# Seven block products instead of eight in the expert layers of a mixture-of-experts stage

## The chip, the core and the metric

The kernel runs on one core of a Trainium2 chip. A core has a matrix engine (TensorE, "PE" in the profile), three engines for elementwise work (VectorE "DVE", ScalarE "ACT", GpSimd "POOL"), a queue that issues transfers (SyncE, "SP") and 16 DMA engines that carry all transfers. Each engine works through its own queue in order and waits there, by semaphores, for what it needs from others. Matmuls read on-chip memory (SBUF) and write accumulators (PSUM); GpSimd does not read PSUM. The metric is the device time in microseconds (us).

## The reference

Inputs: `x` with 4 x 512 tokens of 256 features, one condition vector per sequence. The result is `x` plus a linear attention over the output of a mixture of experts, plus a further branch (attention with a field term, then two layers of local attention and feed-forward). The change touches the experts alone:

```python
gate = xn @ wg_W + wg_b + (genre_embed @ gg_W + gg_b)
gate_w = jax.nn.softmax(gate, axis=-1)
topk_w, topk_i = jax.lax.top_k(gate_w, TOP_K)              # 2 of 8 experts per token
...
h1 = jax.nn.relu(jnp.einsum('bsh,ehm->bsem', x, W1) + b1)    # 256 -> 512
h2 = jax.nn.relu(jnp.einsum('bsem,emn->bsen', h1, W2) + b2)  # 512 -> 512
out_e = jnp.einsum('bsen,enh->bseh', h2, W3) + b3            # 512 -> 256
return jnp.einsum('bseh,bse->bsh', out_e, cw)
```

Everything is 32-bit floating point.

## The kernel before

The kernel computes an expert only for the tokens routed to it. After the gate it sorts the 4096 (token, expert) pairs by expert into **slots**. A slot has one or two blocks of 128 rows of one expert. `SLOTS` gives the order of their sizes: 1, 2, 2, 1, 2, 2, then three times 1, 2, 2, 2, then 1, 2, 2, 1: 22 slots that always run (`often`), 15 of two blocks and 7 of one, numbered here from 0. Two more one-block slots run under a condition and do not run with these inputs. `rowtok` holds for each row of a slot which token to fetch, `goal` which row of the DRAM scratch `ys` its result goes to; rows that hold no token go to row 0 of `ys`, which nobody reads.

For slot j the helpers are:
- `loads` (L1429): SP reads the expert's number and issues three weight loads, `w1` (516 KB, with the biases), `w2` (1024 KB) and `w3` (640 KB, with the output bias). Each has two buffers, so slot j+1's go into those of slot j-1.
- `gather` (L1440): an indirect transfer per block on POOL's queue (L1444) fetches the rows of `x` into `xb`; PE transposes them, ACT or DVE copies them to `xbT`.
- `layer` (L1458): a matrix layer. Weights are the stationary operand in pieces of 128 x 128, tokens the moving operand, 256 wide for two blocks, 128 wide for one. `relu` (L1418) adds the bias and clips at zero on the way out of PSUM, on ACT (L1420) and DVE (L1422) in turn. Each 32-bit product shows in the profile as two weight loads and two matmul instructions, all under L82.
- `last` (L1477): the third layer with the roles exchanged (activations stationary, weights moving, 256 wide), a DVE addition of the output bias (L1483) and an indirect transfer per block on POOL's queue (L1488), which scatters rows to `ys`. As all scatters write `ys`, each waits for the one before it to land.

The loop at L1506 is a software pipeline. Iteration j issues: first layer of j, `last` of j-1, loads and gather of j+1, one weight load for a later stage, second layer of j. Only the transposes and those late loads have a written order (`PE.in_order`, `tc.keep_in_program_order`, "pinned" below); for the rest a planner that knows the dependences chooses each engine's order, and it also moves work of later stages into idle time, such as the additions to `xres` at L1579 and the fills of `v` at L311 and L312, both on POOL. PSUM has four banks for the layers ("mm"), two for transposes, two for the third layer.

After the loop (L1549 on), `ys` is read back and weighted into `y`, four tiles of 128 x 1024 allocated at the start of the kernel and unused until then.

Of the kernel before, what the change touches and what calls it, by code (L numbers as in the profile page):

```python
# [12 lines left out]
F32 = mybir.dt.float32  # L13
I32 = mybir.dt.int32
AF = mybir.ActivationFunctionType
ALU = mybir.AluOpType
# [4 lines left out]
NT = S // 128  # L21
# [21 lines left out]
NRARE = 2  # L43
NROWT = 2 * NPAIR + NHALF
NHI = 2 * NROWT
MCONST = (128, 128 + NE, 2 * NE, 2, NE * NE, NHI, 2 * B * NT, 64, NE)
NMC = sum(MCONST)


# [18 lines left out]
def adaln_attn_ffn_kernel(ctx: ExitStack, tc: tile.TileContext, a: dict, out: bass.AP):  # L68
# [55 lines left out]
    def evac(dst, src):  # L124
        turn[0] ^= 1
        if turn[0]:
            nc.scalar.copy(dst, src)  # L127
        else:
            nc.vector.tensor_copy(dst, src)
# [1032 lines left out]
    with ExitStack() as abc:  # L1162
# [7 lines left out]
        with ExitStack() as moe:  # L1170
# [17 lines left out]
            for n in MCONST:  # L1188
                parts.append(mc[:, at : at + n])
                at += n  # L1190
            mtri, mtiles, mthr, mslot, mlow, miota, mtok, mfold, mwt = parts


            ys = dr.tile([1 + 2 * B * S, H], F32, tag="ys", name="ys")
            xall = a["x"].rearrange("b s h -> (b s) h")


# [201 lines left out]
            pmap2 = acct("pmap2")  # L1399
            for q in range(2):  # L1400
                PE.matmul(pmap2[64 * q : 64 * q + 64, :NROWT], mfold, half_map[:, :, q], start=True, stop=True)
            goal = xp.tile([128, NROWT], I32, tag="goal", name="goal")
            nc.vector.tensor_copy(goal, pmap2[:, :NROWT])
            rowtok = xp.tile([128, NROWT], I32, tag="rowtok", name="rowtok")
            nc.vector.tensor_scalar(rowtok, pmap2[:, :NROWT], -1.0, 0.0, ALU.add, ALU.max)
            nc.vector.tensor_single_scalar(rowtok, rowtok, B * S - 1, op=ALU.bitwise_and)


            def busy(n):
# [7 lines left out]

            def relu(dst, src, bias):  # L1418
                if turn[0]:
                    nc.scalar.activation(dst, src, AF.Relu, bias=bias)  # L1420
                else:
                    nc.vector.tensor_scalar(dst, src, bias, 0.0, ALU.add, ALU.max)  # L1422


            def place(kind, i):
# [11 lines left out]
                d.w3 = ew.tile([128, 5, H], F32, tag="w3", name="w3")  # L1437
                nc.sync.dma_start(d.w3, we[:, 8 + 6 * ME :].rearrange("p (c m) -> p c m", m=H))

            def gather(j, d):  # L1440
                xb = hp.tile([128, 2, H], F32, tag="xb", name="xb", bufs=3)
                for i in range(d.n):
                    r = place(d.n, SLOTS[j][0]) + i
                    nc.gpsimd.indirect_dma_start(  # L1444
                        out=xb[:, i, :], out_offset=None, in_=xall,
                        in_offset=bass.IndirectOffsetOnAxis(ap=rowtok[:, r : r + 1], axis=0))
                n = d.n * 128
                pt = tpt("pxb")
                with PE.in_order():
                    for c in range(2):  # L1450
                        for i in range(d.n):
                            PE.transpose(pt[:, c * n + i * 128 : c * n + (i + 1) * 128],
                                         xb[:, i, c * 128 : (c + 1) * 128], ident)
                xbT = hp.tile([128, 2, 256], F32, tag="xbT", name="xbT")
                evac(xbT[:, :, 0:n], pt[:, : 2 * n].rearrange("p (c t) -> p c t", t=n))
                d.xbT = xbT

            def layer(d, src, tag, w, bias):  # L1458
                n = d.n * 128
# [14 lines left out]
                        relu(dst[:, m, 0:n], ps[:, i * n : (i + 1) * n], d.w1[:, bias + m : bias + m + 1])  # L1474
                return dst

            def last(j, d):  # L1477
                ps = acct("po")
                for i in range(d.n):
                    mm(ps[:, i * H : (i + 1) * H],  # L1480
                       [(d.h2[:, c, i * 128 : (i + 1) * 128], d.w3[:, c, :]) for c in range(4)])
                ob = hp.tile([128, 2, H], F32, tag="ob", name="ob", bufs=3)
                nc.vector.tensor_tensor(  # L1483
                    ob[:, 0 : d.n, :], ps[:, : d.n * H].rearrange("p (i h) -> p i h", h=H),
                    d.w3[:, 4, :].unsqueeze(1).to_broadcast([128, d.n, H]), ALU.add)
                for i in range(d.n):
                    r = place(d.n, SLOTS[j][0]) + i
                    nc.gpsimd.indirect_dma_start(  # L1488
                        out=ys, out_offset=bass.IndirectOffsetOnAxis(ap=goal[:, r : r + 1], axis=0),
                        in_=ob[:, i, :], in_offset=None)  # L1490


            later = {
# [5 lines left out]
            cond_weights(wp, lambda name, load: later.update({name: load}))  # L1499
            cw_ = {}  # L1500

            ds = [SimpleNamespace() for _ in SLOTS]
            loads(0, ds[0])
            gather(0, ds[0])
            often, rare = ds[:-NRARE], range(len(ds) - NRARE, len(ds))
            for j, d in enumerate(often):  # L1506
                if j == len(often) - 1:
                    aside = conditions(cw_, wp)
                    next(aside)
                if j == len(often) - 2:  # L1510
                    halves = nc.values_load(nhalf[0:1, 0:1], min_val=0, max_val=2 * NE)
                if j == 1:
                    weights()
                h1 = layer(d, d.xbT, "h1", d.w1[:, 8:].rearrange("p (c m) -> p c m", m=ME), 0)
                if j:
                    last(j - 1, ds[j - 1])
                if j + 1 < len(often):
                    loads(j + 1, ds[j + 1])
                    gather(j + 1, ds[j + 1])
                    if j > 1 and later:  # L1520
                        name, behind[0] = next(iter(later)), True
                        cw_[name] = later.pop(name)()
                        behind[0] = False
                d.h2 = layer(d, h1, "h2", d.w2, 4)
            last(len(often) - 1, often[-1])

            next(aside)
# [1 line left out]
            with tc.If(halves > NHALF - NRARE):  # L1529
                for j in rare:  # L1530
                    d = ds[j]
                    loads(j, d)
                    gather(j, d)
                    h1 = layer(d, d.xbT, "h1", d.w1[:, 8:].rearrange("p (c m) -> p c m", m=ME), 0)
                    d.h2 = layer(d, h1, "h2", d.w2, 4)
                    last(j, d)
# [213 lines left out]
def _shape_constants():  # L1750
    f = np.float32
    p = np.arange(128)
    bmask = np.repeat((p[:, None] // 32 == p[None, :] // 32).astype(f)[:, None, :], 4, axis=1)
    hmask = np.where(p[:, None] // CHD == np.arange(8)[None, :], CHD**-0.5, 0.0)
    hmask = np.concatenate([hmask, p[:, None] // CHD % 2 == np.arange(2)[None, :]], axis=1).astype(f)
    i, j = p[:, None], p[None, :]
    lmask = np.concatenate([np.where(j >= i, 0.0, MASKED), np.where(j <= i, 0.0, MASKED)], axis=1).astype(f)

    kmask = np.concatenate([(j >= i % 64)[:, :64], (j <= i % 64)[:, :64], j >= i], axis=1).astype(f)

    e = np.arange(NE)
    thr = np.concatenate([256 * e + 128, 256 * e])
    slot = np.full((128, 2), -1)
    slot[: len(SLOTS), 0] = [i if n == 2 else NPAIR + i // 2 for i, n in SLOTS]
    slot[: len(SLOTS), 1] = [-1 if n == 2 else i for i, n in SLOTS]
    tile, expert = p // NE, p % NE
    mconst = np.concatenate(
        [(p[:, None] < p[None, :]).astype(f),
         ((tile[:, None] < tile[None, :]) & (expert[:, None] == expert[None, :])).astype(f),
         (expert[:, None] == e[None, :]).astype(f), np.tile(thr, (128, 1)).astype(f), slot.astype(f),  # L1770
         np.tile((e[None, :] <= e[:, None]).reshape(-1), (128, 1)).astype(f), np.tile(np.arange(NHI), (128, 1)).astype(f),
         (np.arange(2 * B * NT)[None, :] * 128 + p[:, None] + 1).astype(f),
         (p[:, None] % 64 == np.arange(64)[None, :]).astype(f),
         np.tile(np.where(e == NE - 1, 1 - NE, 1), (128, 1)).astype(f)], axis=1)

    pos = np.arange(S, dtype=f)
    inv = f(10000.0) ** np.repeat(np.arange(0, H, 2, dtype=f) / f(H), 2)
    peT = np.ascontiguousarray(np.sin(pos[:, None] / inv[None, :]).astype(f).T)

    half = np.arange(0, DHD, 2, dtype=f)  # L1780
    freqs = pos[:, None] * (f(1.0) / f(10000.0) ** (half / f(DHD)))[None, :]
    base = (half + f(0.4 * DHD)) / f(1.4 * DHD)
    scale = base[None, :] ** ((pos - f(S // 2)) / f(WIN // 2))[:, None]
    cos, sin = np.cos(freqs).astype(f), np.sin(freqs).astype(f)
    parts = []
    for sc in (f(8.0) * scale, f(1.0) / scale):
        c, s = cos * sc, sin * sc
        parts += [np.concatenate([c, c], 1), np.concatenate([-s, s], 1)]
    rot = np.stack(parts).astype(f).reshape(4, NT, 128, DHD).transpose(2, 0, 1, 3)
    return {"mconst": mconst, "bmask": bmask, "hmask": hmask, "lmask": lmask, "kmask": kmask, "peT": peT, "rot": rot}  # L1790
# [81 lines left out]
```

## Time and profile before

| | |
|---|---|
| runs | 1366.4, 1368.9, 1369.9 us; median 1368.9 |
| profiled execution | 1364.1 us; span from first to last instruction 1362.3 us |
| granted TensorE clock over the span | 0.99 |
| busy over the span | PE 1302.8, PEld (weight loads) 850.1, DVE 645.4, ACT 563.9, POOL 227.1 us |
| expert stage | first layer of slot 0 at 42.8 us, last output bias at 313.9 us |
| first and second layer | 1056 matmul instructions (L82, tile `ph`), 43 to 310 us |
| third layer | 296 matmul instructions (tile `po`) |
| gathers, scatters | 37 each |

How to read it: each instruction is put down to the line that made it, with the tile it writes and those it reads (`ph<-h,w`: accumulator `ph` from activations `h` and weights `w`). "Idle before <-X" is the time an engine stood still before an instruction, and what ended that wait. Matmuls overlap: the distance from one start to the next, not the duration of one, is what a matmul costs. A timeline row merges neighbouring instructions of one kind and gives start, length and their number. A stage row ("100.00:150.00") gives each engine's busy time in that stretch, the granted clock, the share of the DMA engines and their rate.

### The profile page before, as it was taken

The numbers are of one execution on the slowest core, as the hardware profiler recorded it, in microseconds if no ns is written. First come the engines' busy times: TensorE is split into PE (matmuls) and PEld (weight loads), VectorE is DVE, ScalarE is ACT, GpSimd is POOL, SyncE is SP. The second block draws the span as 40 slices with busy tenths as digits, with TensorE's granted clock in tenths as the row PEclk, the third lists the DMA queues.
The fourth block names the chain that finished last, engine by engine and source line by source line (L and its number), as shares of the span: only waits on it lengthen the run. The fifth ranks groups of instructions, "written<-read, shape, count | busy, mean of one in ns | idle before, by whom it ended". The sixth has DMA issues, their size and how long they took to land.

```text
span 1362.3 us, 25766 instructions
## 1 busy us (share of the span) xinstructions
PE 1302.8 (96%) x10700; PEld 850.1 (62%) x10700; DVE 645.4 (47%) x1343; ACT 563.9 (41%) x1111; POOL 227.1 (17%) x223
## 2 busy tenths in 40 slices
PE   5899999998999999999999999999999998999998
PEld 4788888884666644444435665766555566667654
DVE  6222212125777743332226777764362767765421
ACT  4111111125555456565655646552223565463111
POOL 1324322211000020010103322100030312210010
PEclk7999999999999999999999999999999999999999
DMA  4577666644000000000201011211001011011000
GB/s 135 205 244 280 228 231 240 211 155 136 1 1 1 0 1 1 1 0 1 90 5 67 13 29 37 81 42 25 24 1 43 24 34 26 19 42 50 20 20 26
DMA packets 43110, 95.02 MB, mean 70 GB/s; under 512 B 9568, under 2 KB 25192, under 8 KB 40168
## 3 DMA queue, kind: packets, MB, share of 16 engines
q1 hardware_dynamic: 37560, 81.81, 18.1%
q0 software_dynamic: 3792, 10.24, 2.2%
q8 instruction: 88, 1.44, 0.4%
q10 hardware_dynamic: 1632, 1.21, 0.3%
q14 instruction: 38, 0.31, 0.1%
HBM read 83.95 MB, written 7.21 MB: 67 GB/s over the span
## 4 chain that ended last, share of the span: by engine, by line
PE 83%; DVE 7%; ACT 6%; issue 2%; DMA 1%; POOL 0%; POOLq 0%; SPq 0%; DVEq 0%; ACTq 0%
PE ph L82 14%; PE pdq L82 10%; PE sc L82 6%; PE pfy L82 6%; PE pug L82 5%; PE pua L82 5%; PE pv L82 5%; PE po L82 5%; PE pdy L82 4%; PE pn L82 3%; PE pz L82 2%; PE pds L82 2%; ACT p L685 2%; PE pqk L82 1%; PE pur L82 1%
## 5 line engine op out<-in xcount | busy, mean ns | idle before, releaser
L82 PE MATMUL pdq<-wqkv,yT 128*128 128x512 f32 x384 | 171.2, 596 | 6.0 <-ACT yT L613 4.1
L425 ACT ACTIVATE cex<-sc 128x512 f32<-128x512 f32 x256 | 131.8, 607 | 84.5 <-PE sc L82 84.4
L82 PE MATMUL ph<-h,w 128*128 128x256 f32 (+1 forms) x704 | 132.8, 346 | 1.6 <-DVE h L1422 1.6
L639 POOL TENSOR_TENSOR qr<-t,t 128x512 f32<-128x512 f32 x64 | 81.3, 1271 | 297.4 <-DVE t L636 282.8
L82 PEld LDWEIGHTS pdq<-wqkv,yT 128*128 128x128 f32 x384 | 71.4, 190 | 90.3 <-issue 76.9
L82 PEld LDWEIGHTS ph<-h,w 128*128 128x128 f32 x704 | 116.1, 191 | 13.7 <-DVE h L1422 1.9
L1420 ACT ACTIVATE h<-ph,w 128x256 f32<-128x256 f32 (+1 forms) x88 | 35.3, 437 | 190.9 <-PE ph L82 130.5
L1422 DVE TENSOR_SCALAR h<-ph,w 128x256 f32<-128x256 f32 (+1 forms) x88 | 36.1, 438 | 161.1 <-PE ph L82 102.6
L685 ACT ACTIVATE p<-pds,ss 128x192 f32<-128x192 f32 (+1 forms) x256 | 82.3, 434 | 12.5 <-PE pds L82 11.2
L82 PE MATMUL sc<-qm,kT 32*128 32x512 f32 x512 | 86.8, 639 | 0.0
L629 ACT ACTIVATE sq<-pdq 128x512 f32<-128x512 f32 x64 | 38.4, 601 | 97.1 <-POOL qr L639 50.2
L82 PE MATMUL pug<-hT,w 128*128 128x512 f32 x160 | 75.9, 597 | 0.0
L82 PE MATMUL pua<-hT,w 128*128 128x512 f32 x160 | 75.2, 592 | 0.0
L82 PE MATMUL ph<-xbT,w 128*128 128x256 f32 (+1 forms) x352 | 68.7, 347 | 0.5 <-ACT xbT L127 0.5
L82 PE MATMUL po<-w,h 128*128 128x256 f32 x296 | 67.6, 379 | 0.0
L395 POOL TENSOR_SCALAR fterm<-vw,faT 128x256 f32<-128x256 f32 x16 | 14.6, 922 | 312.1 <-DVE cr L385 259.6
L789 ACT ACTIVATE gl<-pug,cols 128x512 f32<-128x512 f32 x40 | 27.3, 687 | 86.5 <-PE pug L82 86.4
L82 PEld LDWEIGHTS ph<-xbT,w 128*128 128x128 f32 x352 | 58.5, 191 | 7.2 <-ACT xbT L127 0.7
L82 PE MATMUL pfy<-w,uA 128*128 128x256 f32 x256 | 61.2, 382 | 0.0
L82 PEld LDWEIGHTS pn<-p,v 64*64 64x64 f32 x1792 | 44.1, 136 | 27.4 <-issue 10.1
L82 PE MATMUL pv<-cex,v 128*32 128x512 f32 x512 | 61.2, 597 | 0.0
L82 PEld LDWEIGHTS po<-w,h 128*128 128x128 f32 x296 | 55.7, 190 | 8.1 <-ACT h L1420 0.9
(304 smaller groups left out, 2182.7 us busy)
## 6 DMA issues: line engine op xcount, KB each, us to landing
w<-in_moe_w_dram SPq DMA_DIRECT2D x22, 1024.0 KB
w<-in_moe_w_dram SPq DMA_DIRECT2D x22, 640.0 KB
w<-in_moe_w_dram SPq DMA_DIRECT2D x22, 516.0 KB
zb<-rows SPq DMA_DIRECT2D x32, 256.0 KB
g<-ys SPq DMA_DIRECT2D x6, 512.0 KB
wqkv<-in_f_wqkv_dram SPq DMA_DIRECT2D x2, 1536.0 KB
w<-in_f_w_dram SPq DMA_DIRECT2D x2, 1408.0 KB
out_dram<-yc SPq DMA_DIRECT2D x16, 128.0 KB
```

What stands on the lines that cost most here:

```text
L82: cls._queue(nc.tensor.matmul(*args, **kw))
L395: nc.gpsimd.tensor_scalar_mul(fterm[:, t, :], vw, W["faT"][:, t, b : b + 1])
L425: nc.scalar.activation(ex[:, i, :], pss[2 * j + i], AF.Exp, scale=CHD**-0.5)
L629: nc.scalar.activation(sq, p3, AF.Square)
L639: nc.gpsimd.tensor_tensor(qr_t[:, s], t1, t2, ALU.add)
L685: nc.scalar.activation(p[:, at : at + n], pss[j // 2][r][:, at % 384 : at % 384 + n], AF.Exp, scale=d.ss[:, j, 1, 2 * c + r : 2 * c + r + 1])
L789: nc.scalar.activation(gl, pg, AF.Gelu, bias=col("bg", l * (NU + 1) + i))
L1420: nc.scalar.activation(dst, src, AF.Relu, bias=bias)
L1422: nc.vector.tensor_scalar(dst, src, bias, 0.0, ALU.add, ALU.max)
```

## The change

In 14 slots (those of two blocks except slot 1; the flag is `few`) the first two layers are computed as a 2 x 2 block product with seven block products instead of eight. Weights are cut in halves along both their sides (a11, a12, a21, a22), activations likewise (b11 to b22, with 128 tokens each). Four sums of weight blocks are made on POOL (`weight_sums`), four sums of token blocks on DVE (`token_sums`), and the seven products, each 128 wide, are combined by seven additions on DVE out of PSUM (`plus`), one copy on ACT and eight halves of bias and relu on ACT, now out of SBUF. The sums live in the four `y` tiles, one set for each layer: a set is written again for each slot.

The order of the loop changes too, and is now written out on PE, POOL and, for the slots' work, ACT and DVE. Iteration j issues: first layer of j (and the token sums of its result), loads of j+1, first-layer weight sums of j+1, gathers of j+2, `last` of j-1 with its scatters, transposes of j+1 (and their token sums), second layer of j, second-layer weight sums of j+1. Rows without a token are scattered to 128 rows of their own at the end of `ys`, one for each partition.

```diff
-            ys = dr.tile([1 + 2 * B * S, H], F32, tag="ys", name="ys")
+            ys = dr.tile([1 + 2 * B * S + 128, H], F32, tag="ys", name="ys")
...
-            goal = xp.tile([128, NROWT], I32, tag="goal", name="goal")
-            nc.vector.tensor_copy(goal, pmap2[:, :NROWT])
             rowtok = xp.tile([128, NROWT], I32, tag="rowtok", name="rowtok")
...
+            nc.vector.scalar_tensor_tensor(goalf, pmap2[:, :NROWT], 0.0, maside.to_broadcast([128, NROWT]),
+                                           ALU.is_equal, ALU.mult)
+            goal = xp.tile([128, NROWT], I32, tag="goal", name="goal")
+            nc.vector.tensor_tensor(goal, pmap2[:, :NROWT], goalf, ALU.add)
...
+            def weight_sums(s, w):
+                n = w.shape[1] // 2
+                a11, a12, a21, a22 = (w[:, j0 * n : (j0 + 1) * n, 256 * i0 : 256 * i0 + 256]
+                                      for i0 in range(2) for j0 in range(2))
+                pinned(nc.gpsimd.tensor_tensor(s[0], a21, a22, ALU.add))
+                pinned(nc.gpsimd.tensor_tensor(s[1], s[0], a11, ALU.subtract))
+                pinned(nc.gpsimd.tensor_tensor(s[2], a11, a21, ALU.subtract))
+                pinned(nc.gpsimd.tensor_tensor(s[3], a12, s[1], ALU.subtract))
+
+            def token_sums(src):
...
+                pinned(nc.vector.tensor_tensor(t[:, 0], b12, b11, ALU.subtract))
+                pinned(nc.vector.tensor_tensor(t[:, 1], b22, t[:, 0], ALU.subtract))
+                pinned(nc.vector.tensor_tensor(t[:, 2], b22, b12, ALU.subtract))
+                pinned(nc.vector.tensor_tensor(t[:, 3], b21, t[:, 1], ALU.subtract))
+                return t
+
+            def layer_few(d, src, t, tag, w, s, bias):
...
+                ps = [mmt("ph").rearrange("p (k m t) -> p k m t", k=2, m=2) for _ in range(4)]
...
+                def product(k, lhs, rhs):
+                    for m in range(2):
+                        mm(ps[k // 2][:, k % 2, m], [(lhs[m][c], rhs[:, c]) for c in range(n)])
+                    return ps[k // 2][:, k % 2]
+
+                def block(i0, j0, out, p, other):
+                    plus(out, p, other)
+                    for m in range(2):
+                        pinned(nc.scalar.activation(
+                            dst[:, 2 * i0 + m, 128 * j0 : 128 * j0 + 128], out[:, m], AF.Relu,
+                            bias=d.w1[:, bias + 2 * i0 + m : bias + 2 * i0 + m + 1]))
+
+                def plus(out, p, other):
+                    pinned(nc.vector.tensor_tensor(out, p, other, ALU.add))
+
+                p1 = product(0, whole(0, 0), src[:, 0:n, 0:128])
+                pinned(nc.scalar.copy(e1, p1))
+                p6 = product(1, summed(1), t[:, 1])
+                plus(e16, p6, e1)
+                p2 = product(2, whole(0, 1), src[:, n : 2 * n, 0:128])
+                block(0, 0, e1, p2, e1)
+                p5 = product(3, summed(0), t[:, 0])
+                plus(e15, p5, e16)
+                p7 = product(4, summed(2), t[:, 2])
+                plus(e17, p7, e16)
+                block(1, 1, e16, p5, e17)
+                p3 = product(5, summed(3), src[:, n : 2 * n, 128:256])
+                block(0, 1, e15, p3, e15)
+                p4 = product(6, whole(1, 1), t[:, 3])
+                block(1, 0, e17, p4, e17)
+                return dst
...
-                h1 = layer(d, d.xbT, "h1", d.w1[:, 8:].rearrange("p (c m) -> p c m", m=ME), 0)
-                if j:
-                    last(j - 1, ds[j - 1])
-                if j + 1 < len(often):
-                    loads(j + 1, ds[j + 1])
-                    gather(j + 1, ds[j + 1])
-                    if j > 1 and later:
...
-                d.h2 = layer(d, h1, "h2", d.w2, 4)
+                with PE.in_order():
+                    if d.few:
+                        h1 = layer_few(d, d.xbT, d.t1, "h1", w1, d.s1, 0)
+                        t2 = token_sums(h1)
+                    else:
+                        h1 = layer(d, d.xbT, "h1", w1, 0)
+                    if j + 1 < len(often):
+                        loads(j + 1, after)
+                        if later and j > 1:
...
+                    if after.few:
+                        first_sums(after)
+                    if j + 2 < len(often):
+                        fetch(j + 2, ds[j + 2])
+                    if j:
+                        last(j - 1, ds[j - 1])
+                    if j + 1 < len(often):
+                        turn_tokens(after)
+                    d.h2 = layer_few(d, h1, t2, "h2", d.w2, d.s2, 4) if d.few else layer(d, h1, "h2", d.w2, 4)
+                if after.few:
+                    second_sums(after)
```

## The prediction

> **What bounds the kernel now.** I read the page's first part, then stage sums over the expert stage (42.8 to 314 us), then the timelines of the engines that the change touches.
>
> ```profile
> PE 1302.8 (96%) x10700; PEld 850.1 (62%) x10700; DVE 645.4 (47%) x1343; ACT 563.9 (41%) x1111; POOL 227.1 (17%) x223
> ```
>
> The share of a stage matters more:
>
> ```profile
> core 0: us, PE busy (x) PEld busy (x) DVE busy (x) ACT busy (x) POOL busy (x), PEclk, DMA share, GB/s
> 100.00:150.00 50.00, 50.00 (x264) 44.64 (x263) 10.29 (x23) 7.46 (x18) 24.57 (x21) 1.00 0.74 258
> 150.00:200.00 50.00, 50.00 (x263) 44.66 (x262) 10.28 (x23) 7.45 (x18) 13.68 (x14) 1.00 0.66 229
> 200.00:250.00 50.00, 50.00 (x264) 44.64 (x263) 10.29 (x23) 7.46 (x18) 13.71 (x14) 1.00 0.66 233
> ```
>
> PE has no idle time here: the stage is as long as its matmul stream, and what leaves that stream leaves the time unless something else then ends last. PE's timeline gives the spacing of matmuls:
>
> ```profile
> 163.16 1.95 PE L82 MATMUL ph<-xbT,w 128*128 128x128 f32 x16
> 164.94 3.62 PE L82 MATMUL po<-w,h 128*128 128x256 f32 x16
> 168.84 3.74 PE L82 MATMUL ph<-h,w 128*128 128x128 f32 x32
> 172.41 3.62 PE L82 MATMUL ph<-xbT,w 128*128 128x256 f32 x16
> 178.03 7.07 PE L82 MATMUL ph<-h,w 128*128 128x256 f32 x32
> 184.94 0.38 PE L82 MATMUL ph<-xbT,w 128*128 128x256 f32 x1
> ```
>
> From start to next start, 32 matmuls 256 wide take 6.91 us (0.216 each; each product is two instructions) and 32 that are 128 wide take 3.57 us (0.1116 each). Half the width costs half; the weight load does not show. The engine that gains most work is POOL; its timeline:
>
> ```profile
> 72.06 1.00 POOL L1488 DMA_INDIRECT ys<-ob,goal  x1 [0.30 <-issue]
> 81.20 0.98 POOL L1488 DMA_INDIRECT ys<-ob,goal  x1 [8.13 <-DMA ys<-ob,goal]
> ...
> 120.50 0.99 POOL L1488 DMA_INDIRECT ys<-ob,goal  x1 [0.30 <-issue]
> 126.64 0.97 POOL L1488 DMA_INDIRECT ys<-ob,goal  x1 [5.15 <-DMA ys<-ob,goal]
> 127.62 6.98 POOL L1579 TENSOR_TENSOR xres<-xres,crows 128x1024 f32<-128x1024 f32 x3
> 134.54 1.80 POOL L311 MEMSET v<- 128x2048 f32 x1
> ```
>
> The second scatter of a two-block slot sits in the queue until the first has landed: 9.1 us from one issue to the next at 72, 6.1 at 120. POOL also does 9.1 us of later stages' work here (L1579, L311, L312), which drifted into its idle time.
>
> **The change part by part.** All in us.
>
> *PE.* Fourteen slots (all 256-row ones but slot 1) change. First layer: 16 x 0.216 = 3.46 becomes 7 products x 2 x 2 instructions = 28 x 0.1116 = 3.12. Second: 32 x 0.216 = 6.91 becomes 56 x 0.1116 = 6.25. That is 0.99 a slot, **-13.9** in all, on the path.
>
> *DVE and ACT.* Removed: eight evictions of 0.47 a slot, four on each engine. Added on DVE: 14 sums out of PSUM (0.415, the row L738/L825 with the same operands) 5.8, four token sums of 128x128 (0.283, L691) 1.1, four of 128x256 (0.416, L1391) 1.7; with the output bias 0.69 that is 9.3. ACT: 2 copies (0.37) and 16 halves of relu (0.367) and the token copy 0.585, 7.2. PE's 13.3 a slot covers both: **0**. In the first layer alone ACT has 3.3 against PE's 3.12; the 3.9 of output layer and transposes behind it hide that. Without this cover the second layer would start about 2.3 later (last sum, two relus, the first token sums).
>
> *Gathers two ahead, order of the queues.* PE waited 1.2 in all for gathers: at most that, taken as 0. The row table now comes out before the scatter table, one DVE copy (L1403, 0.20) earlier at the start of the stage: **-0.2**. The two added table operations end long before the first scatter at 58. SP's order of loads is as before: the third weight still waits for the output layer's reads. Pinned POOL order becomes: four first-layer weight sums, gathers, scatters, four second-layer weight sums.
>
> *POOL.* These are the prices:
>
> ```profile
> L639 POOL TENSOR_TENSOR qr<-t,t 128x512 f32<-128x512 f32 x64 | 81.3, 1271 | 297.4 <-DVE t L636 282.8 <-PE pdy L82 13.5 <-PE pds L82 1.0
> ...
> L396 POOL TENSOR_TENSOR fterm<-fterm,crows 128x256 f32<-128x256 f32 x16 | 11.3, 725 | 0.0
> ```
>
> A slot adds 4 x 0.725 = 2.90 and 4 x 1.271 = 5.08. A gather or scatter takes 1.26 from issue to next issue. A scatter's landing holds POOL longer: the gap from first to second scatter is 3.5 to 3.9 after a two-block slot, and 6.1, 5.2, 4.5, 4.8 (mean 5.15) in the iterations of one-block slots (at 120, 170, 220, 269). Over four slots (1, 2, 2, 2 blocks) POOL has 3 x 7.98 + 14 x 1.26 + extra waits (5.15 + 3.8 + 3.8 - 3 x 1.26) = 50.5; PE, with a halved output layer of 1.73, has 9.26 + 11.54 + 13.27 + 13.05 = 47.1, where before it had 50.1. **POOL becomes the bound.**
>
> Where it bites: a one-block slot j before a two-block slot j+1. Count from the start of j's first layer (163.16 for slot 10). The next first weight is issued at 164.28, when its buffer is free, and its 4128-byte packets end at 167.9: 4.75. Then POOL needs 2.90 for first sums, 2.52 for two gathers, 5.15 from scatter to scatter, 1.26 for the second, and 2.54 for the two second-layer sums behind the second product: 19.1. PE gets there after 1.79 + 3.46 + 0.44 + 3.57 (slot j), 3.12 + 1.73 + 0.44 (j+1) and the first product, 0.89: 15.4. So PE waits 3.7 at slots 4, 7, 11, 15 and 19; everything behind that weight load in PE's queue waits too. Five times 3.7 is **+18.3**. It agrees with 50.5 - 47.1 = 3.4 a cycle. Bounds by the gap: at 3.5, the shortest with a next slot to come, 2.0 x 5 = +10.2; at 6.6 (88.48 to 95.05, with weights in flight) 5.1 x 5 = +25.6. I take the one-block iterations' own mean, as the wait is in these.
>
> *DVE and POOL together.* The token sums read two tensors in SBUF while POOL adds. The nearest rows:
>
> ```profile
> 1145.47 5.08 DVE L732 TENSOR_TENSOR oT<-oT,zb 128x512 f32<-128x512 f32 x2
> ...
> 1147.33 2.67 POOL L778 TENSOR_TENSOR yc<-yc,xres 128x1024 f32<-128x1024 f32 x1
> ```
>
> Two DVE products of 0.68 each took 5.1 beside POOL's additions, and POOL's own took 2.67 where the other three took 2.34 to 2.35. Yet all 64 of L639 took 1.26 to 1.28, so POOL is mostly not held up. For POOL I bound a transition by 0 and 8 x 0.28 = 2.2; I take two of the eight, 0.56 x 5 = **+2.8** (bounds 0 to +11). The skill's rule speaks against the change more strongly: by the Trainium skill, "SBUF — State Buffer", section Who interferes with whom, a VectorE instruction with two SBUF inputs and a GpSimd one that reads SBUF exclude each other, and whichever issues second fully blocks. By that rule all eight would count and this term would be about +14; by L639's rows it would be 0.
>
> *PE's clock.* Idle gaps of 2.35 (322.8 to 325.1) and 3.06 (1148.1 to 1151.1) were each followed by 3.41 at half clock, gaps up to 1.85 by none. Each such window costs 1.7; for half of five waits of 3.7: **+4.3** (0 to +8.5).
>
> *Drifted POOL work.* The 9.1 of L1579, L311 and L312 is not pinned behind the new work and may still land inside a queue that is now full, or at its end: half, **+4.5** (0 to +9.1).
>
> Sum: -13.9 - 0.2 + 18.3 + 2.8 + 4.3 + 4.5 = +15.8. On the profiled execution's own 1364.1 (span 1362.3) that makes 1379.9; the median of the runs, 1368.9, is 4.8 above it, so **1384.7**. About 0.3% is what a measurement here can tell from no change.
>
> **Rivals.**
> *Scatters land sooner (faster).* The change sends unused rows to 128 spare rows instead of all to row 0; if that, or the later place of the scatters, shortens the gap, the chain fits. Decisive is a gap of 4.3: then the wait is 2.8 x 5 = 14.1, the whole gain, extras aside. At 3.5 with no extras: -14.1 + 10.2 = -3.9, 1365; with no wait between scatters at all the chain takes 15.2, PE never waits: 1354.8. For it: three pairs at 3.5 to 3.8. Against it: pairs in one-block iterations never went under 4.5.
> *DVE becomes the bound (slower still).* If all eight token sums of a slot wait out a POOL addition (1.0, the mean of 0.725 and 1.271), DVE has 9.3 + 8.0 = 17.3 a slot against PE's 13.3: -14.1 + 14 x 4.0 = +42, 1411; if six of eight do, 15.3 and +14, 1383. At four of eight it is 13.3 and costs nothing. Against it: POOL is in transfers and their waits for five or more of 13 us, when no sums meet.
> *Break-even.* A gap near 4.3 and no extras: 1365 to 1373.
>
> **How the numbers follow.** POOL's chain binds with extras: 0.57 (own range +5 to +30). Scatters land sooner: 0.20. DVE bound: 0.10. Break-even: 0.13. The low end, 1358, leaves out the no-wait limit of the first rival; the high end, 1404, holds the gap of 6.6 with the taken extras (-14.1 + 25.6 + 11.6 = +23, 1392) and the lower part of the DVE case. Faster 0.20, same 0.13, slower 0.67.
>
> **What would show it.** PE's matmuls in the layers at 0.11 spacing, 28 and 56 a slot; POOL near full over the whole expert stage; PE's waits in the second layer of slots 4, 7, 11, 15, 19 put down to POOL's sums, some 3 to 4 each; token sums far over 0.42. The forecast is wrong if POOL has idle time left before its second-layer sums, if the second scatter no longer waits, or if PE's waits name DVE or ACT.

## The result, and the profile after

The changed kernel takes **1468.7 us** (median; 1463.7 to 1477.2) against 1368.2 of the kernel before beside it: a ratio of 1.074, 95% interval 1.069 to 1.080. The forecast was 1384.7 with a range of 1358 to 1404. The sign was right; the loss is 100 us instead of 16, far outside the range.

The profiled execution spans 1468.8 us. From the first layer's first matmul to the start of the last output layer's last matmul ("the stage" below) it needs 372.9 us, where the kernel before needed 270.7: 102.2 of the 106.5 that the spans differ by. Of the other 4.3, 0.3 lie ahead of the stage and 4.0 behind it; what takes them stays open. Part 1 of the page, and the clock's row of part 2 (one digit for each 36.7 us), after:

```profile
PE 1335.5 (91%) x11204; PEld 886.1 (60%) x11204; DVE 760.3 (52%) x1585; ACT 632.4 (43%) x1318; POOL 340.0 (23%) x335
...
PEclk8999797979999999999999999999999999999999
```

The sums by stretch, after (each engine's busy time and its instructions in brackets, then the granted clock, the share of the DMA engines and their rate):

```profile
core 0: us, PE busy (x) PEld busy (x) DVE busy (x) ACT busy (x) POOL busy (x), PEclk, DMA share, GB/s
100.00:150.00 50.00, 38.41 (x266) 35.15 (x266) 24.54 (x54) 15.15 (x43) 25.83 (x27) 0.97 0.56 189
150.00:200.00 50.00, 39.05 (x227) 35.19 (x228) 22.77 (x45) 13.78 (x40) 38.39 (x34) 0.83 0.42 143
200.00:250.00 50.00, 40.14 (x233) 36.74 (x232) 24.48 (x48) 13.96 (x40) 27.84 (x29) 0.80 0.47 156
```

PE, which had no idle time in these stretches before, now stands still for a fifth of them, and its clock falls to 0.80. No other engine is anywhere near full: the most is POOL's 38.4 of 50. So by these sums no engine is short of time; PE waits for single results. The waits of PE in the stage, after (total, number, longest):

```profile
PE ph L82 <- DVE e L1546: 35.6, 55, 2.6
PE ph L82 <- POOL ymoe L1501: 16.6, 6, 3.8
PE ph L82 <- issue: 10.0, 13, 1.1
PE ph L82 <- ACT e L1549: 6.9, 7, 1.1
```

L1501 is the second weight sum, the one named in the prediction. But the first, third and fourth line were in no step of it. L1546 is `plus` (DVE adds a product out of PSUM to an earlier sum), L1549 the copy of product 1 by ACT. PE's timeline over one two-block slot, after (start, length, what, how many, and the idle time ahead with its releaser):

```profile
138.84 0.61 PE L82 MATMUL ph<-xbT,w 128*128 128x128 f32 x4
140.55 0.68 PE L82 MATMUL ph<-t,ymoe 128*128 128x128 f32 x4 [1.10 <-issue]
141.07 0.61 PE L82 MATMUL ph<-xbT,w 128*128 128x128 f32 x4
142.35 1.16 PE L82 MATMUL ph<-t,ymoe 128*128 128x128 f32 x8 [0.67 <-DVE e L1546]
144.12 0.68 PE L82 MATMUL ph<-xbT,ymoe 128*128 128x128 f32 x4 [0.61 <-DVE e L1546]
144.64 0.61 PE L82 MATMUL ph<-t,w 128*128 128x128 f32 x4
145.09 1.89 PE L82 MATMUL po<-w,h 128*128 128x256 f32 x8
146.81 0.60 PE L86 MATMUL pxb<-ident,xb 128*128 128x128 f32 x4
147.25 1.06 PE L82 MATMUL ph<-h,w 128*128 128x128 f32 x8
152.11 1.16 PE L82 MATMUL ph<-ymoe,ymoe 128*128 128x128 f32 x8 [3.80 <-POOL ymoe L1501]
```

The first six rows are the seven products of the first layer. PE waits before the 2nd, the 4th and the 6th, and before no other. The 2nd product's operands had long been there; in the same trace ACT reads product 1 just then:

```profile
140.09 0.36 ACT L1549 COPY e<-ph 128x256 f32<-128x256 f32 x1
```

It ends at 140.45, and PE starts at 140.55. `product(k)` writes to `ps[k // 2][:, k % 2]`: products 0 and 1 share a PSUM bank, as do 2 and 3, 4 and 5. The second of a pair waits until the first has been read out. Three waits in each of 28 layers are 84; the profile lists 75 under DVE, ACT and "issue", and seven under POOL's sums (L1501, L1502). In distances from start to start, what PE's matmuls in the stage take at these waits beyond their spacing (0.216 or 0.1116) is 84.9 us, against 3.0 before (such a sum is good to about 2). Less POOL's 16.6, about 68 lie at the pairs.

The clock makes up a third part. Two neighbouring stretches, after:

```profile
214.00:225.00 11.00, 6.48 (x44) 5.71 (x44) 7.51 (x16) 4.25 (x12) 4.25 (x5) 1.00 0.70 218
225.00:238.70 13.70, 11.43 (x50) 10.88 (x51) 6.32 (x10) 2.09 (x6) 12.77 (x13) 0.50 0.21 74
```

In the first, PE runs 6.5 of 11 us, in bursts between waits of 0.6 to 1.1, and a wait of 3.1 begins at its end; the next 13.7 us are granted half speed. The stage has eight windows at half speed, of 3.4 to 13.7 us each; PE's work in them took 25.3 us longer.

The account: PE's own saving -13.9, waits +81.9, half clock +25.3 make +93.3 of the 102.2. Of the 9 left, the rows above show where most would lie: four matmuls take 0.68 rather than 0.61 after a wait, which makes 6 over some 85 waits. The rest is open.

### The profile page after: what moved, and what is told of

It reads as the page before. It is cut to its first block, busy times and chain, and to the rows that moved or that the text cites. A ratio compares the mean times of both kernels' runs of the same rounds, so it can differ in the third digit from the quotient of the medians.

```text
span 1468.8 us, 27483 instructions
## 1 busy us (share of the span) xinstructions
PE 1335.5 (91%) x11204; PEld 886.1 (60%) x11204; DVE 760.3 (52%) x1585; ACT 632.4 (43%) x1318; POOL 340.0 (23%) x335
## 4 chain that ended last, share of the span: by engine, by line
PE 57%; DVE 6%; ACT 5%; issue 3%; DMA 2%; POOL 0%; SPq 0%; ACTq 0%; DVEq 0%; POOLq 0%
PE pdq L82 8%; PE sc L82 6%; PE pfy L82 5%; PE pug L82 5%; PE pua L82 5%; PE pv L82 5%; PE pdy L82 4%; PE pn L82 3%; PE pz L82 2%; PE pds L82 2%; ACT p L685 1%; PE pqk L82 1%; PE pcy L82 1%; PE pf L82 1%; PE pck L82 1%
## 5 line engine op out<-in xcount | busy, mean ns | idle before, releaser
L1546 DVE TENSOR_TENSOR e<-ph,e 128x256 f32<-128x256 f32 x196 | 83.2, 424 | 125.8 <-PE ph L82 122.4
L1541 ACT ACTIVATE h<-e,w 128x128 f32<-128x128 f32 x224 | 76.5, 393 | 163.2 <-DVE e L1546 161.6
L82 PE MATMUL ph<-ymoe,ymoe 128*128 128x128 f32 x336 | 54.1, 321 | 29.1 <-POOL ymoe L1501 15.5
L629 ACT ACTIVATE sq<-pdq 128x512 f32<-128x512 f32 x64 | 38.4, 601 | 97.5 <-POOL qr L639 50.7
L82 PE MATMUL po<-w,h 128*128 128x256 f32 x296 | 71.8, 396 | 0.0
L82 PEld LDWEIGHTS ph<-ymoe,ymoe 128*128 128x128 f32 x336 | 48.4, 227 | 34.6 <-POOL ymoe L1501 16.4
L82 PE MATMUL ph<-h,w 128*128 128x128 f32 (+1 forms) x480 | 66.4, 291 | 0.0
L1576 POOL DMA_INDIRECT ys<-ob,goal x37 | 36.6, 990 | 124.7 <-DMA ys<-ob,goal 68.6
L82 PEld LDWEIGHTS ph<-h,w 128*128 128x128 f32 x480 | 62.1, 200 | 1.4 <-ACT h L1423 0.3
L82 PE MATMUL pn<-p,v 64*64 64x128 f32 (+1 forms) x1792 | 51.4, 256 | 10.8 <-DVE p L688 9.9
```

What stands on the lines that cost most here:

```text
L82: cls._queue(nc.tensor.matmul(*args, **kw))
L629: nc.scalar.activation(sq, p3, AF.Square)
L1541: pinned(nc.scalar.activation(dst[:, 2 * i0 + m, 128 * j0 : 128 * j0 + 128], out[:, m], AF.Relu, bias=d.w1[:, bias + 2 * i0 + m : bias + 2 ...
L1546: pinned(nc.vector.tensor_tensor(out, p, other, ALU.add))
L1576: pinned(nc.gpsimd.indirect_dma_start(out=ys, out_offset=bass.IndirectOffsetOnAxis(ap=goal[:, r : r + 1], axis=0), in_=ob[:, i, :], in_off ...
```

## The experiments

Times are medians; "stage" and "waits" are the two sums defined above, from each kernel's profiled execution (the waits good to about 2), and "half clock" is what PE's work lost to windows at half speed; a blank has no sum. Each ratio is against the kernel before beside it, whose medians lie between 1366.2 and 1369.9. The kernels without weight or token sums leave out work, and their outputs are not the reference's.

| kernel | us | ratio (95%) | stage | waits | half clock |
|---|---|---|---|---|---|
| before | 1368.2 | 1 | 270.7 | 3.0 | 0 |
| after | 1468.7 | 1.074 (1.069 to 1.080) | 372.9 | 84.9 | 25.3 |
| e1_banks | 1405.9 | 1.027 (1.025 to 1.029) | 310.1 | 41.1 | 13.2 |
| e2_banks_nosums | 1365.3 (one run) | | 268.6 | 10.6 | 2.8 |
| e3_order_only | 1367.9 | 0.999 (0.997 to 1.001) | 270.5 | | |
| e4_nosums | 1443.9 (one run) | | 346.0 | 72.7 | 10.9 |
| e5_banks_late | 1377.4 | 1.009 (1.006 to 1.012) | 280.3 | 22.6 | |
| e6_second_layer | 1371.8 | 1.004 (1.003 to 1.005) | 274.3 | 12.3 | |
| e7_second_late | 1358.0 | 0.993 (0.991 to 0.996) | 262.8 | 4.1 | |
| e9_late_notokens | 1380.6 (one run) | | 277.6 | 18.8 | 4.1 |
| e10_late_pinned | 1377.0 | 1.007 (1.005 to 1.009) | 273.1 | | 0 |
| e11_second_pinned | 1363.4 | 0.997 (0.996 to 0.998) | 261.0 | 1.3 | |
| e12_pinned_notokens | 1374.5 (one run) | | 269.8 | 13.7 | |
| e13_second_late_again | 1359.3 | 0.992 (0.990 to 0.993) | 262.7 | | |

### Shared banks against POOL's sums

**e1_banks** puts products four apart into one bank, so that neighbours in time have different banks; nothing else differs.

```diff
-                        mm(ps[k // 2][:, k % 2, m], [(lhs[m][c], rhs[:, c]) for c in range(n)])
-                    return ps[k // 2][:, k % 2]
+                        mm(ps[k % 4][:, k // 4, m], [(lhs[m][c], rhs[:, c]) for c in range(n)])
+                    return ps[k % 4][:, k // 4]
```

> The seven products of a layer are laid out so that those which share a PSUM bank are four apart (first and fifth, second and sixth, third and seventh) instead of neighbours. Nothing else changes. Theory A (bank pairs): in the changed kernel PE waits before the second, fourth and sixth product of each of the 28 layers until the neighbour in the same bank has been read out, about 0.7 us each, some 60 us, and the clock falls to half because of these gaps, 25 us. Then this layout takes away 60 to 85 us: 1385 to 1410 us. Theory B (POOL is the bound, as forecast, and the short waits only fill time that PE has to wait anyway): the waits move to POOL's sums and the time stays within 10 us of the changed kernel, 1455 to 1475 us.

**e4_nosums** is the changed kernel without weight sums, **e2_banks_nosums** has the edit of e1 as well.

```diff
-                pinned(nc.gpsimd.tensor_tensor(s[0], a21, a22, ALU.add))
...
-                pinned(nc.gpsimd.tensor_tensor(s[3], a12, s[1], ALU.subtract))
+                s[:] = [w[:, j0 * n : (j0 + 1) * n, 256 * i0 : 256 * i0 + 256]
+                        for i0 in range(2) for j0 in range(2)]
```

> The changed kernel without the sums of weight blocks on POOL (plain weight blocks in their place, so the outputs are not the reference's), with the products paired in banks as in the change. Theory A: only POOL's waits go, 20 to 25 us and some of the half clock: 1425 to 1450 us. Theory B: nearly everything goes: 1355 to 1380 us.

> The layout of the first kernel of this set, and the sums of weight blocks on POOL are left out: the products take plain weight blocks of the same shape in their place, so the outputs are not the reference's, and POOL has only gathers and scatters. Theory A: what is left beside the banks are POOL's 20 to 25 us of waits; without both the expert stage is 14 us shorter than before at best: 1352 to 1370 us. Theory B gives the same here. If it stays above 1380, a third cause (DVE, ACT or the order of the queues) holds PE.

**e3_order_only** sets the flag `few` to False for all slots: the order of the loop, the gathers two ahead and the spare rows stay, the block products go.

> The new order of the loop, the gathers two slots ahead and the spare rows stay, but no slot uses the block products: every layer is computed as before the change. If the order costs nothing by itself (both theories): within 6 us of the kernel before, 1362 to 1375 us. If the written-out order takes freedom that the planner used: above 1378 us.

Measured: the four kernels with block products form a square.

| us | weight sums | none |
|---|---|---|
| pairs share a bank | 1468.7 | 1443.9 |
| products four apart share one | 1405.9 | 1365.3 |

The banks alone are worth 62.8 with the sums and 78.6 without, the sums 24.8 with shared banks and 40.6 without. The two don't add up, because a wait at a bank gives POOL time to finish (waits at L1501 are 16.6 with shared banks, 30.3 without). With both gone the kernel is at 1365.3, 4.2 under the kernel before in the same comparison; the stage, less its waits and half clock, is 255.2, where the kernel before less its waits and PE's predicted 13.9 is 253.8. So the saving on PE is there, and it is the waits that bury it (e2 and e4 are one run each). PE's timeline of e1, at the same seven products:

```profile
128.18 0.61 PE L82 MATMUL ph<-xbT,w 128*128 128x128 f32 x4
128.62 0.61 PE L82 MATMUL ph<-t,ymoe 128*128 128x128 f32 x4
129.07 0.61 PE L82 MATMUL ph<-xbT,w 128*128 128x128 f32 x4
129.97 1.16 PE L82 MATMUL ph<-t,ymoe 128*128 128x128 f32 x8 [0.29 <-DVE h L1425]
130.96 0.61 PE L82 MATMUL ph<-xbT,ymoe 128*128 128x128 f32 x4
131.41 0.61 PE L82 MATMUL ph<-t,w 128*128 128x128 f32 x4
...
141.86 2.08 PE L82 MATMUL ph<-ymoe,ymoe 128*128 128x128 f32 x8 [6.02 <-POOL ymoe L1501]
```

The seven run through at 0.45 for four, the spacing that the prediction used. PE's waits in e1's stage:

```profile
PE ph L82 <- POOL ymoe L1501: 30.3, 6, 6.2
PE pxb L86 <- DMA xb<-in_x_dram,rowtok: 2.1, 3, 0.9
PE ph L82 <- DVE e L1546: 1.6, 2, 1.4
```

The waits for DVE's additions fall from 35.6 to 1.6; POOL's are now nearly all. In e4 it is the other way round, and no wait is put down to POOL:

```profile
PE ph L82 <- DVE e L1542: 30.4, 54, 1.0
PE ph L82 <- ACT e L1545: 19.7, 26, 1.1
```

e3 is within its interval of the kernel before: order, early gathers and spare rows together cost and bring nothing that can be told from no change.

### POOL's chain

e1's POOL timeline at the wait of 6.02:

```profile
130.37 1.00 POOL L1576 DMA_INDIRECT ys<-ob,goal  x1 [0.30 <-DVE e L1546]
138.18 0.99 POOL L1576 DMA_INDIRECT ys<-ob,goal  x1 [6.81 <-DMA ys<-ob,goal]
139.19 1.28 POOL L1500 TENSOR_TENSOR ymoe<-w 128x512 f32<-128x512 f32 x1
140.54 1.26 POOL L1501 TENSOR_TENSOR ymoe<-ymoe,w 128x512 f32<-128x512 f32 x1
```

POOL stands still for 6.8 until the first scatter has landed, then issues the second, then makes the two sums; 141.80 is their end, 141.86 PE's start. This is the chain as the prediction told it. The wait for the landing doesn't come from the sums, though. e3, which has none, shows it too:

```profile
119.12 1.01 POOL L1576 DMA_INDIRECT ys<-ob,goal  x1 [3.23 <-DVE ob L1571]
126.67 0.98 POOL L1576 DMA_INDIRECT ys<-ob,goal  x1 [6.54 <-DMA ys<-ob,goal]
```

There PE isn't held up, as no product waits for POOL's sums.

**e5_banks_late** takes the gap out of the chain: e1, with the second scatter of a slot issued behind the second-layer sums.

```diff
+                d.ob = ob
+                scatter(j, d, 0)
...
                 if after.few:
                     second_sums(after)
+                if j:
+                    scatter(j - 1, ds[j - 1], 1)
```

> As e1_banks, with one move on POOL's queue: the second scatter of a slot is issued after the second-layer weight sums instead of straight behind the first, so that POOL no longer stands still while the first lands. Same instructions, same sums. Theory A2 (what is left of e1_banks' loss is POOL's chain: weight load, first sums, gathers, 7 us from scatter to scatter, second sums): the sums then end before PE needs them, 30 us of waits on POOL and most of the 13 us of half clock go: 1357 to 1372 us. Theory B2 (POOL's sums themselves are too much, with the port shared with DVE and later stages' work on POOL): only some 10 us go, 1390 to 1400 us.

Measured: 28.5 less than e1 (25.3 when each is taken against the kernel before beside it), and the stage 29.8 less, where e1's waits for L1501 were 30.3. That lies between the two expectations. What is left is 9.6 above the stage before, and its largest piece is new. e5's timeline:

```profile
129.75 7.41 DVE L1513 TENSOR_TENSOR t<-xbT 128x128 f32<-128x128 f32 x1
...
130.06 6.94 POOL L1693 TENSOR_TENSOR xres<-xres,crows 128x1024 f32<-128x1024 f32 x3
...
138.77 1.62 PE L82 MATMUL ph<-h,ymoe 128*128 128x128 f32 x6 [7.00 <-DVE e L1546]
```

A token sum that takes 0.28 alone lasts 7.4 beside the three drifted additions to `xres`, and PE waits 7.0 for the DVE work queued behind it.

**e6_second_layer** leaves the first layer as before (no first-layer sums, e1's banks); **e7_second_late** is e6 with the second scatter moved as in e5.

```diff
-                if d.few:
-                    d.t1 = token_sums(d.xbT)
...
-                        h1 = layer_few(d, d.xbT, d.t1, "h1", w1, d.s1, 0)
+                        h1 = layer(d, d.xbT, "h1", w1, 0)
...
-                    if after.few:
-                        first_sums(after)
```

> The layout of e1_banks, and block products in the second layer alone: the first layer is computed as before the change, its weight and token sums go. PE saves 14 x 0.66 = 9.3 us instead of 13.9; POOL loses 2.9 us a slot and the wait for the first weight load. Theory A2: the chain after a one-block slot is third-layer output 6.2, 7 from scatter to scatter, 1.3, 2.5 = 17.0 us against PE's 15.8: five waits of 1.2, 1362 to 1370 us. Theory B2: 1375 to 1390 us.

> As e6_second_layer, with the second scatter behind the second-layer weight sums as in e5_banks_late. Theory A2: no wait on POOL is left, PE's 9.3 us stay: 1358 to 1364 us. Theory B2 (sums and DVE's shared port cost by themselves): 1368 us or more.

Measured: e6 is 0.4% slower than before, a little over the 1362 to 1370 expected; e7 is 0.7% faster. e7's stage is 7.9 shorter than before. PE alone should save 14 x (6.91 - 6.25) = 9.2, and waits went from 3.0 to 4.1: 8.1. The sums by stretch, e7:

```profile
150.00:200.00 50.00, 50.00 (x345) 46.88 (x344) 21.01 (x50) 15.23 (x41) 32.20 (x30) 1.00 0.70 241
200.00:250.00 50.00, 50.00 (x345) 46.88 (x344) 21.63 (x51) 15.23 (x41) 30.27 (x28) 1.00 0.73 250
```

PE is full again at full clock. e6's waits beyond that (6.8 for the second weight sum, 3.0 for token sums) go with the scatter's place.

### What holds the version with both layers

**e9_late_notokens** is e5 without token sums, to see whether DVE beside POOL is what costs.

```diff
-                pinned(nc.vector.tensor_tensor(t[:, 0], b12, b11, ALU.subtract))
...
-                return t
+                return (b12, b22, b12, b21)
```

> e5_banks_late without the sums of token blocks on DVE: the products take plain token blocks in their place, so the outputs are not the reference's. Theory C (what is left in e5_banks_late, some 20 us of PE's waits, comes from DVE's token sums, which read two tensors in SBUF and stand still while POOL adds, one of them 7.4 us behind later stages' additions to xres): 1352 to 1362 us. Theory D (POOL's own queue is still late): above 1370 us.

**e10_late_pinned** is e5 with the `xres` additions held in written order behind the stage (the fills of `v` go with them); **e11_second_pinned** the same edit on e7.

```diff
-                nc.gpsimd.tensor_tensor(
-                    xres[b], xres[b], row("bo").unsqueeze(1).to_broadcast([128, NT, H]), ALU.add)
+                tc.keep_in_program_order(nc.gpsimd.tensor_tensor(
+                    xres[b], xres[b], row("bo").unsqueeze(1).to_broadcast([128, NT, H]), ALU.add))
```

> e5_banks_late with the three drifted additions to xres and two fills of v put behind the expert stage on POOL's queue; nothing else changes. Theory C: the 7 us wait at 131 to 139 us goes, with the half clock it brings: 5 to 8 us less than e5_banks_late, 1369 to 1373 us. Theory D: POOL is ahead by its 9.1 us, PE waits less on its sums: 9 us less or more, 1368 us or below; if the additions then delay the next stage: no gain.

> e7_second_late with the same work put behind the expert stage. It had one wait of 2.2 us on POOL, next to these additions: 1 to 2 us less, 1355 to 1358 us; if the additions then delay the next stage, which begins with them: no gain, 1358 to 1362 us.

**e12_pinned_notokens** joins both edits; **e13_second_late_again** is e7 once more with more rounds.

> e10_late_pinned without the sums of token blocks (plain token blocks in their place, so the outputs are not the reference's). If the token sums are what holds PE in e10_late_pinned (DVE waits 6.3 and 2.6 us by its profile, and the 5 or so under them), its expert stage of 273.1 us loses 8 to 14 us: 259 to 265, which is within 6 us of the old stage less the 13.9 us of saved matmuls (256.8). If the stage stays above 268 us, POOL's queue is still late by itself.

> e7_second_late once more, in more rounds. Its profile shows an expert stage of 262.8 us against 270.7 before, and nothing lost behind it: 1357 to 1362 us, 0.4 to 0.8% less than the kernel before. If its first measurement was a lucky one: within 0.3% of before, as e11_second_pinned was.

Measured: without token sums (e9) the stage is 2.7 shorter than e5's, but the time isn't less: PE then waits 7.5 for the second weight sum of a first layer, behind the drifted work, and 6.7 for gathers. So e5's wait of 7.0 that named DVE goes back to the same drifted work. Pinning (e10) takes 7.2 out of the stage, about the 7.0 wait shown above, and all its half clock; yet the time stays within the intervals of e5's, and the stretch behind the stage grows by 5.2 (from the last output layer to the next stage's first products 15.4 instead of 13.1, the stage after it 161.1 instead of 158.2, with half clock at 328 to 335 and 345 to 352). On e7 the same edit loses: 1363.4 instead of 1358.0 and 1359.3. With both gone (e12) the stage is 269.8, 13.0 above what PE alone would need (270.7 - 13.9 = 256.8). PE's largest wait in it:

```profile
PE pxb L86 <- DMA xb<-in_x_dram,rowtok: 8.6, 5, 2.5
```

These are gathers that come late. The longest of them left POOL's queue at 136.12, behind four weight sums that ended at 134.70, and PE started at 143.31; whether the late issue or the landing weighs more, no run tells. So the reading that the token sums were what held e5 falls: without them the stage is 3.3 shorter, where 8 to 14 were expected. POOL isn't full of work either, with 37 to 38 of each 50 us; it stands still for transfers. Its two largest waits in e12:

```profile
POOL ys L1572 <- DMA ys<-ob,goal: 28.4, 11, 5.1
POOL ymoe L1500 <- DMA w<-in_moe_w_dram: 25.1, 4, 11.6
```

In e7, which has 2.9 less of sums a slot and no sums that wait for the first weight, the waits for gathers are one of 1.0, as in the kernel before. What sets the 269.8 was not tried by itself and stays open.

e13 repeats e7's gain (ratio 0.990 to 0.993). The second layer alone, with banks apart and the second scatter late, is 8 us (e7) and 11 us (e13) below the kernel before beside it. What e5 has beyond e7, block products in the first layer, costs more than it saves.

## Why the prediction was wrong, point by point

**PE, -13.9: right.** Products run at 0.1116 a matmul (e1's rows), and with waits and half clock taken off e2's stage comes within 1.4 of it.

**"DVE and ACT ... PE's 13.3 a slot covers both: 0": the step that failed.** It added up busy times and compared sums. DVE and ACT did fit into PE's slot (24.5 and 15.2 of 50 us), but the order within a layer decides: of two products in one bank the second waits for the first to end, for its reader to start, and for 0.36 to 0.42 of reading. That is an idle time of 0.5 to 1.2 in nearly every case, some 68 in the stage counted from start to start; e1, which changes the bank index and nothing else, takes 62.8 off the time. The prediction asked only what lies at the end of a layer ("the second layer would start about 2.3 later") and not where each accumulator lies; its list of what would prove it wrong did name these waits ("if PE's waits name DVE or ACT"). The code gave it: `ps[k // 2][:, k % 2]`, with a reader between k even and k odd. By the Trainium skill, "PSUM — Partial Sum Buffer", section PSUM bank collisions raise a hardware error, PSUM is to be guarded by bank and quadrant rather than by address, since two engines on one bank collide on disjoint columns too. The waits in the trace follow that rule: product 2's columns were free, and PE waited all the same. No run tells whether the chip would have needed the wait; all show that this kernel has it.

**POOL's chain, +18.3: right in mechanism, too small.** Place and order are as told: five waits at the second product of the second layer, at L1501 (a sixth, of 1.1, stands in a first layer). That the changed kernel's 16.6 comes near 18.3 is luck: the gap was longer than thought, and bank waits gave POOL time. e1, where bank waits don't cover it, shows 30.3, of which 26.7 are the five and 3.6 a first layer. The term that was mis-sized is the gap between scatters, taken as 5.15: in the five one-block iterations of e1 it is 7.1, 7.8, 5.8, 5.8 and 7.7, mean 6.8, and 7.0 in the changed kernel. With 6.8 the same count gives (3.7 + 1.7) x 5 = 27. Part of this lay in the kernel before: the 5.15 leaves out the first of the five such iterations, the pair at 88.48 with 6.57 that the prediction has as its upper bound; with it the mean is 5.4. In the changed kernel SP issues weights at 140.60 and 141.18, and the scatter leaves at 140.77; that the weights make the landing slow is argued from this, no run took them away. It can't be all: in e3 only the third weight leaves beside the scatter (118.87 and 119.12; in the kernel before 119.25 and 120.50), the others 4.7 behind it, and the five gaps are 5.3 to 7.6, mean 6.3. So the new order or the spare rows lengthen them without any sums; no run took these two apart. POOL was never "near full" (26 to 38 of 50): its queue was late because it stood still.

**DVE and POOL together, +2.8: near, by luck.** POOL's 56 sums of 512 took 1.291 in the mean instead of 1.271, those of 256 0.752 instead of 0.725, 2.6 in all. But the term priced five transitions, and by these means the four sums of 256 and two of 512 in each lost some 0.7 together. (Its two prices for the rule don't agree either: 8 x 0.28 gives the bound of +11, four at 0.283 and four at 0.416 the +14.) The delay fell on the other side. Groups of the changed kernel (busy us, mean ns, then idle before):

```profile
L1514 DVE TENSOR_TENSOR t<-xbT,t 128x128 f32<-128x128 f32 x14 | 12.2, 875 | 0.5
...
L1501 POOL TENSOR_TENSOR ymoe<-ymoe,w 128x256 f32<-128x256 f32 x14 | 10.5, 750 | 1.0
```

Token sums of 128x128, taken as 0.283, have a mean of 0.58 to 0.88 by line, those of 128x256, taken as 0.416, of 0.48 to 0.62. The skill's rule, which would have cost POOL 14, isn't borne out for POOL here; for DVE it is nearer, up to the 7.4 beside three additions. The rival "DVE becomes the bound" wanted more than four of eight sums held up for 1.0; all of them together lost 29 us over 14 slots, 2.1 a slot, and DVE has room. Taking the token sums out was worth 2.7 in the stage (e9 against e5) and 3.3 (e12 against e10).

**PE's clock, +4.3: too small by 21.** It was counted as one short window behind each long wait. Five of the eight windows do come with such a wait, of 2.6 to 3.8; the other three begin 3.4 after the window before, with gaps of 0.6 to 1.1 alone. In the changed kernel, with short gaps all around, four waits of 3.1 to 3.8 were followed by 3.4 once and by 10.2 to 13.7 at half clock three times; in e1, which has few short gaps, waits of 3.6 and 3.8 were followed by 3.4 each, and longer ones of 4.5 to 6.2 by 6.8 to 10.2. Short gaps can also do it alone, as twice in e4, where nothing over 1.06 lies in the 20 us ahead of the window:

```profile
236.00:247.70 11.70, 8.43 (x67) 7.48 (x65) 4.80 (x13) 3.82 (x12) 3.92 (x4) 1.00 0.45 124
247.70:254.50 6.80, 6.28 (x22) 5.50 (x23) 3.55 (x9) 2.67 (x8) 0.00 (x0) 0.50 0.47 196
```

Mostly they don't: four stretches of 48 to 55 us between the changed kernel's windows are full of them and stay at full clock. So the loss doesn't go with the sum of the waits: e4 has 72.7, with one wait of 6.0 among many short ones, and loses 10.9; e1 has 41.1, nearly all in six long ones, and loses 13.2; e10, whose longest wait is 1.9, loses none. By the Trainium skill, "TensorE: Matmul & The Clock Gate", section A second HAM failure mode: psum-queue depth-cycling, PE can idle briefly between groups of matmuls often enough for the clock to swing between half and full. The stretches above swing so; what decides whether a series of short gaps does it, no run shows.

**Drifted POOL work, +4.5.** It did land in the full queue: 6.98 at 154.46 in the changed kernel. e10 prices it at 7.2 in the stage and at nothing in the whole: the work then stands behind the stage, where the time grows.

**Order and gathers, -0.2: not contradicted** (e3, 0.999; its interval can't tell 0.2 from nothing). The rival "scatters land sooner" fell: gaps got longer, in e3 too. "Break-even" fell with it.

## What to carry to other kernels

Before work beside the matmuls is costed at nothing because its sum fits, follow one round through the accumulators: which bank each product writes, who reads the bank's neighbour, and whether PE's next instruction stands behind that read. Products that follow each other belong in different banks. An in-order queue that holds both compute and transfers passes every landing time on to the compute, so the transfer that must wait goes last, and waits of PE are to be priced with the clock that they take away, long ones above all.

## What the runs showed of the hardware that was not expected

- Waits of 3.1 to 3.8 us were followed by up to 13.7 us at half clock where gaps of 0.6 to 1.1 lay all around them (changed kernel), and waits of 3.6 and 3.8 by 3.4 where few did (e1); in the kernel before, single gaps of 2.35 and 3.06 were followed by 3.4. Twice in e4, gaps of at most 1.06 were followed by 6.8.
- From the issue of one scatter to the next took 5.6 to 7.8 us in the one-block iterations of the changed kernel and e1, and 5.3 to 7.6 in e3, where it had been 4.5 to 6.6 in the kernel before.
- A DVE subtraction of 128x128 with both operands in SBUF, 0.28 in other places, took 7.41 beside three POOL additions of 6.94 together, which were not longer than in the kernel before (6.98).
